# Reordering the last stage of a graph-attention layer with residual norm

## The chip, the cores and the metric

The kernel runs on one core of a Trainium2 chip. The core has TensorE (PE in the profile, with its weight loads as PEld), VectorE (DVE), ScalarE (ACT), GpSimd (POOL) and SyncE (SP), which here only issues transfers; 16 DMA engines move the data. The metric is the device time of one execution in microseconds. Before the change it is 236.07 us (median of 3 runs, 235.55 to 236.43).

## The reference

`x` is 4096 x 512, `adj` 4096 x 4096, both 32-bit floats. The layer is attention with four heads over the rows of `x`, with `adj` added to the scores, the mean over the heads, a residual and a norm over each row:

```python
ht = (h @ W).reshape(N, N_HEADS, N_HIDDEN).transpose(1, 0, 2)
...
e = jax.nn.leaky_relu(src[:, :, None] + dst[:, None, :], SLOPE) + adj_mat[None]
att = jax.nn.softmax(e, axis=-1)
h_prime = jnp.einsum('hij,hjd->hid', att, ht)
return h_prime.mean(axis=0)
...
x = _layernorm(x + _L0_gnn_ref(x, adj, L0_gnn_W, L0_gnn_a), axis=-1)
```

The entries of `adj` that are not zero go up to 1e9, so that in a row the largest entry decides the softmax by itself when it leads the second largest by more than the scores can differ. For such a row the result is `norm(x[i] + x[j] @ mean_h(W_h))`, where `j` is the column of the row's largest `adj`.

## The kernel before

The kernel computes that short form for all rows (`leading_rows`), bounds the scores from the norms of `x` and of the projected weights, counts the rows in which the lead is too small, and runs a full attention (`general`) only if there are any. With these inputs there are none, so the time is that of `leading_rows`.

The 4096 rows are 32 blocks of 128 rows, one row per partition. `NB` is 32, `KB` (parts of 128 of the 512 columns) is 4, `Q` is 4, `LATE` is 28 and `BEHIND` is 24. The schedule is written by hand: the order of the calls is the order on each engine's queue, and only semaphore waits are added to it.

A block passes these stages in the loop over `t`:

- `load_adj`: SP fetches the block's 2 MB of `adj`, five blocks ahead; the last block comes in four pieces. All loads and stores are on SP's queue, in the order of the calls, with at most eight under way.
- `segment_maxima`, `find_segment`: VectorE takes the maximum of each segment of 32 columns, then the largest segment maximum and its segment. GpSimd works out the segment's place (`row`, L174), gathers the segment from `adj` by an indirect transfer (`lead`, L176) and keeps the segment's first column (`start`, L181).
- `find_column`, two steps later: VectorE finds the column within the segment (L198), GpSimd adds the start (`col`, L200) and gathers the row of `x` for each partition (`y`, L186, in `gather_rows`). Block 31 doesn't go by its segment: `find_column_in_row` searches the whole row of 4096 (L206).
- `turn`, one step after that: TensorE transposes `y` in four parts (L213), ScalarE copies the result out of PSUM (`yt`, L215). `products` multiplies it by the mean of the heads' weights, four matmuls of 128x512 (L228), accumulating in PSUM.
- The residual. Up to block 23, `residual` (L221) adds `x` by a matmul with the identity, in the same PSUM tile. Blocks 24 to 27 are put by in SBUF (`put_by`, L241), and `add_x` (L244) adds their `x` later. Blocks 28 and 29 have a residual matmul at the start of step 31, and block 30 gets its `x` from VectorE (L511). Block 31 is kept as two half tiles, with `residual_in_halves` (L266) and `products_of_half` (L270).
- The norm. Either ScalarE makes the sums (`stats`, L250 and L252), GpSimd the inverse deviation (`rstd`, L255 to L257) and ScalarE the result (`finish`, L261), or, for the late blocks, VectorE makes `moments` (L281, L285), ScalarE a square root (L287), VectorE the inverse (`factor`, L290, L292) and the result (`normalise`, L297).

What is left after the loop is written out call by call (L463 to L525): the `x` norms of blocks 24 to 27 and ten stores of finished blocks, the search for blocks 30 and 31, then the products of blocks 28 to 31 between the norms of blocks 24 to 31 and the score bound (`bound(0)` to `bound(3)`, `test`, `count`, `report`), with the last six stores at the end. `store` is L313. A store of four blocks moves 8 KB per partition, one of two blocks 4 KB.

Of the kernel before, what the change touches and what calls it, by code (L numbers as in the profile page):

```python
# [10 lines left out]
U32 = mybir.dt.uint32  # L11
# [55 lines left out]
def leading_rows(ctx, tc, x, adj, W, a, out, ident, v, n_bad, any_bad):  # L67
# [100 lines left out]
    def find_segment(ib):  # L168
        seg = seg_of.pop(ib)
        nc.vector.max(out=top[:, ib, :], in_=seg)  # L170
        at = small.tile([P, 8], U32, name="at")
        nc.vector.max_index(at, top[:, ib, :], seg)  # L172
        row = small.tile([P, 1], U32, name="row")
        nc.gpsimd.tensor_tensor(row, at[:, 0:1], first[:, ib : ib + 1], op=OP.add)  # L174
        lead = lead_pool.tile([P, E], F32, name="lead")
        nc.gpsimd.indirect_dma_start(  # L176
            out=lead, out_offset=None, in_=adj_segs,
            in_offset=bass.IndirectOffsetOnAxis(ap=row[:, :1], axis=0),
        )
        start = at_of[ib] = small.tile([P, 1], U32, name="start")  # L180
        nc.gpsimd.tensor_tensor(start, at[:, 0:1], width, op=OP.mult)  # L181
        lead_of[ib] = lead

    def gather_rows(ib, col):
        y = y_t[ib] = y_pool.tile([P, D], F32, name="y")
# [8 lines left out]
    def find_column(ib):  # L194
        if ib < BEHIND:
            find_inner(ib)
        within = small.tile([P, 8], U32, name="within")
        nc.vector.max_index(within, top[:, ib, :], lead_of[ib])  # L198
        col = small.tile([P, 1], U32, name="col")
        nc.gpsimd.tensor_tensor(col, at_of.pop(ib), within[:, 0:1], op=OP.add)  # L200
        gather_rows(ib, col)
# [7 lines left out]
    def turn(ib):  # L209
        y = y_t.pop(ib)  # L210
        tp = psum.tile([P, KB, P], F32, name="tp", bufs=2)
        for kb in range(KB):
            nc.tensor.transpose(tp[:, kb, :], y[:, ts(kb, P)], ident)  # L213
        yt = yt_of[ib] = rows.tile([P, KB, P], F32, name="yt")
        nc.scalar.copy(yt, tp)  # L215

    def residual(ib):
        start = ib not in o_ps
        if start:
            o_ps[ib] = psum.tile([P, D], F32, name="o")  # L220
        nc.tensor.matmul(o_ps[ib], ident, hold[:, ib, :], start=start, stop=False)  # L221

    def products(ib, lo=0, hi=KB):
        start = ib not in o_ps
        if start:
            o_ps[ib] = psum.tile([P, D], F32, name="o")
        for kb in range(lo, hi):
            nc.tensor.matmul(  # L228
                o_ps[ib], yt_of[ib][:, kb, :], w_sum[:, kb, :],
                start=(start and kb == 0), stop=(kb == KB - 1),  # L230
            )
# [11 lines left out]
    def add_x(engine, ib):  # L243
        engine.tensor_add(hold[:, ib, :], hold[:, ib, :], o_ps["by"][:, ib - BEHIND, :])  # L244
        o_ps[ib] = hold[:, ib, :]

    def stats(ib):
        o, i = o_ps[ib], slice(ib, ib + 1)
        sq = rows.tile([P, D], F32, name="sq")
        nc.scalar.activation(sq, o, AF.Identity, scale=-1.0 / D, accum_out=nm[:, i])  # L250
        sq = rows.tile([P, D], F32, name="sq")
        nc.scalar.activation(sq, o, AF.Square, bias=nm[:, i], accum_out=sd[:, i])  # L252
# [6 lines left out]
    def finish(ib):  # L259
        i = slice(ib, ib + 1)  # L260
        nc.scalar.activation(hold[:, ib, :], o_ps.pop(ib), AF.Identity, bias=nm[:, i], scale=sd[:, i])  # L261

    def residual_in_halves(ib):
        o_ps[ib] = [psum.tile([P, D // 2], F32, name="o") for _ in range(2)]
        for k, o in enumerate(o_ps[ib]):
            nc.tensor.matmul(o, ident, hold[:, ib, ts(k, D // 2)], start=True, stop=False)  # L266
# [10 lines left out]
    def moments(ib):  # L277

        if ib < NB - 1:
            st = small.tile([P, nc.vector.BN_STATS_DIM], F32, name="st", bufs=2)  # L280
            nc.vector.bn_stats(st, o_ps[ib])  # L281
        else:
            st = halves_st
        mv = mean_var[ib] = small.tile([P, nc.vector.BN_AGGR_DIM], F32, name="mv", bufs=3)
        nc.vector.bn_aggr(mv, st)  # L285
        r = rt[ib] = sd[:, ib : ib + 1]
        nc.scalar.activation(r, mv[:, 1:2], AF.Sqrt, bias=eps)  # L287

    def factor(ib, shift=False):
        nc.vector.reciprocal(rt[ib], rt[ib])  # L290
        if shift:
            nc.vector.scalar_tensor_tensor(  # L292
                nm[:, ib : ib + 1], mean_var[ib][:, 0:1], -1.0, rt[ib], op0=OP.mult, op1=OP.mult
            )
# [17 lines left out]
    def store(queue, lo, n):  # L312
        queue.dma_start(out_rows[:, ds(lo, n), :], hold[:, ds(lo, n), :])  # L313
# [90 lines left out]
    vectors = [(kb, h) for kb in range(KB) for h in range(H)]  # L404
    vectors_at = {t: 2 if t < 3 else 1 for t in range(1, 15)}
    COLUMN, PROJECT, STATS, FINISH = 2, 3, 4, 6

    for t in range(NB):
        if t == NB // 2:
            tc.mark_branch_hint_location("general", engines=HINTED)  # L410
        if t in x_at:
            load_x(*x_at[t])
        if t + AHEAD == NB - 1:
            load_x(LATE, Q)
        load_adj(t + AHEAD)
        middle = 1 if t == NB - 1 else 2
        segment_maxima(t, 0, middle)
        if t >= COLUMN:
            find_column(t - COLUMN)
        segment_maxima(t, middle, PIECES)  # L420
        pair = FINISH <= t < BEHIND + FINISH and t % 2 == 0
        if pair:
            rstd(slice(t - FINISH, t - FINISH + 2))
        if t == NB - 1:
            for ib in (BEHIND, BEHIND + 2):
                load_x(ib, 2)
        find_segment(t)
        if t < 2:
            mean_of_heads(t)
        elif t == 2:  # L430
            mean_of_heads(2)
            mean_of_heads(3)
        if t == 0:
            turn_a()
        turned = [(*vectors[0], turn_w(*vectors.pop(0))) for _ in range(vectors_at.get(t, 0))]
        if t == 16:
            head_norms()
        ib = t - PROJECT
        if t == NB - 1:
            for late in range(LATE, NB):  # L440
                row_norm(late)
            residual(LATE)
            residual(LATE + 1)
        if ib >= 0:
            turn(ib)
            if ib > BEHIND:
                products(ib - 1, KB - 1, KB)
            if ib < BEHIND:
                residual(ib)
        for some in turned:  # L450
            head_vector(*some)
        if ib >= 0:
            products(ib, 0, KB if ib < BEHIND else KB - 1)
        if t >= BEHIND + STATS:
            put_by(t - STATS)
        elif t >= STATS:
            stats(t - STATS)
            row_norm(t - STATS)
        if pair:
            finish(t - FINISH)  # L460
            finish(t - FINISH + 1)

    for ib in range(BEHIND, LATE):  # L463
        row_norm(ib)
    for ib in range(0, 2 * Q, Q):
        store(nc.sync, ib, Q)
    for ib in range(2 * Q, BEHIND, 2):
        store(nc.sync, ib, 2)
    find_column(NB - 2)
    add_x(nc.gpsimd, BEHIND)  # L470
    add_x(nc.gpsimd, BEHIND + 1)
    find_column_in_row(NB - 1)
    add_x(nc.gpsimd, BEHIND + 2)
    products(LATE, KB - 1, KB)
    residual_in_halves(NB - 1)
    turn(NB - 3)
    products(NB - 3, 0, KB - 1)
    moments(LATE)
    for ib in range(BEHIND, NB):
        find_inner(ib)  # L480
    bound(0)
    products(NB - 3, KB - 1, KB)
    stats(BEHIND)
    factor(LATE)
    normalise(LATE, o_ps.pop(LATE))
    bound(1)
    turn(NB - 2)
    bound(2)
    add_x(nc.vector, LATE - 1)
    stats(BEHIND + 1)  # L490
    moments(LATE - 1)
    products(NB - 2, 0, 2)
    bound(3)
    test()
    pg = count()
    products(NB - 2, 2, KB - 1)
    stats(BEHIND + 2)
    rstd(slice(BEHIND, BEHIND + 2))
    rstd(slice(BEHIND + 2, BEHIND + 3))
    moments(NB - 3)  # L500
    report(pg)
    turn(NB - 1)
    factor(LATE - 1, shift=True)
    factor(NB - 3)
    normalise(NB - 3, o_ps.pop(NB - 3))
    finish(BEHIND)
    finish(BEHIND + 1)
    products(NB - 2, KB - 1, KB)
    products_of_half(NB - 1, 0)
    products_of_half(NB - 1, 1)  # L510
    nc.vector.tensor_add(hold[:, NB - 2, :], o_ps[NB - 2], hold[:, NB - 2, :])  # L511
    o_ps[NB - 2] = hold[:, NB - 2, :]
    moments(NB - 2)
    stats_of_half(NB - 1, 0)
    factor(NB - 2)
    normalise(NB - 2, o_ps.pop(NB - 2))
    finish(BEHIND + 2)
    finish(BEHIND + 3)
    stats_of_half(NB - 1, 1)
    moments(NB - 1)  # L520
    factor(NB - 1, shift=True)
    finish_in_halves(NB - 1)
    for ib, n in ((NB - 4, 1), (NB - 3, 1), (BEHIND, 2), (NB - 2, 1), (BEHIND + 2, 2)):
        store(nc.sync, ib, n)
    store(nc.sync, NB - 1, 1)  # L525

# [152 lines left out]
```

## Time and profile before

| | us |
|---|---|
| median of 3 runs | 236.07 |
| lowest, highest | 235.55, 236.43 |
| the profiled execution | 236.21 |
| its span, first to last instruction | 234.6 |
| PE busy (matmul) | 195.2 |
| DVE busy | 188.4 |
| ACT busy | 111.6 |
| POOL busy | 101.2 |

The span is the time between the first and the last instruction of the profiled execution; its own time has 1.6 us more, before and after it. Bytes moved: 97.21 MB, 414 GB/s over the span. The costliest groups of the page, with count, busy time and mean of one, then the idle time of the engine before them and who ended it:

```profile
L163 DVE TENSOR_REDUCE seg<-adj_t 128x64 f32<-128x2048 f32 (+1 forms) x68 | 146.0, 2149 | 32.7 <-DMA adj_t<-in_adj_dram 32.3
L228 PE MATMUL o<-w_sum,yt 128*128 128x512 f32 x248 | 115.1, 605 | 1.7 <-ACT yt L215 1.7
L176 POOL DMA_INDIRECT lead<-in_adj_dram,row x32 | 32.3, 1010 | 15.5 <-POOL row L174 15.0
L186 POOL DMA_INDIRECT y<-in_x_dram,col x32 | 30.9, 965 | 15.4 <-POOL col L200 15.2
```

A 128x512 matmul of 32-bit floats appears as two passes, so counts of L228 and its like are twice the calls. Matmuls overlap, so 605 ns is the length of one pass's record and not what one pass costs in a row of them.

### The profile page before, as it was taken

Reading aid. Unit: us, or ns where it says so; the run is one execution under the profiler, and the core shown is the slowest. Engines: PE = TensorE matmul, PEld = TensorE weight load, DVE = VectorE, ACT = ScalarE, POOL = GpSimd, SP = SyncE. Lnnn points to the kernel's source line nnn. Section 1 sums busy time; section 2 is a strip of 40 time slices with the busy share of each in tenths; the row PEclk is TensorE's granted clock in tenths of the full one; section 3 lists DMA queues with packets and bytes.
Section 4 is the critical chain, followed back from the end, with each engine's and each line's share of the span. In section 5 each row is a group of like instructions: output and inputs, shape, how many; then the busy total and the mean of one; then the engine's idle time right before and its main releaser. Section 6 shows DMA issues by size and latency. Waiting matters only on the chain.

```text
span 234.6 us, 2498 instructions
## 1 busy us (share of the span) xinstructions
PE 195.2 (83%) x683; PEld 101.4 (43%) x683; DVE 188.4 (80%) x302; ACT 111.6 (48%) x267; POOL 101.2 (43%) x215
## 2 busy tenths in 40 slices
PE   0188929999999999999979879797998968698990
PEld 0034514756565655555534333242443423244460
DVE  1736875589869995999589989998799999989672
ACT  2012011255474747474758354646464645166582
POOL 1012232414527462646353645464365464549130
PEclk9999977999999999999999999999799999999998
DMA  6999999999999999999999999999999999999985
GB/s 226 439 428 426 443 425 430 415 440 412 440 420 426 424 437 434 425 424 428 427 432 433 425 433 422 432 418 429 425 432 418 422 425 427 411 425 419 417 355 210
DMA packets 13697, 97.21 MB, mean 414 GB/s; under 512 B 2152, under 2 KB 2664, under 8 KB 7792
## 3 DMA queue, kind: packets, MB, share of 16 engines
q1 hardware_dynamic: 10080, 88.08, 88.9%
q0 software_dynamic: 3584, 8.92, 9.6%
q8 instruction: 6, 0.10, 0.2%
q14 instruction: 11, 0.09, 0.1%
q10 hardware_dynamic: 16, 0.02, 0.0%
HBM read 88.62 MB, written 8.39 MB: 414 GB/s over the span
## 4 chain that ended last, share of the span: by engine, by line
DMA 45%; POOL 17%; issue 15%; PE 10%; DVE 9%; ACT 1%; POOLq 0%; SPq 0%; DVEq 0%
DMA adj_t<-in_adj_dram 42%; DVE seg L163 8%; PE o L228 7%; POOL lead L176 6%; POOL y L186 5%; DMA y<-in_x_dram,col 3%; POOL sd L256 2%; PE o L270 2%; POOL start L181 1%; POOL row L174 1%; POOL col L200 1%; PE tp L213 1%; PE o L221 1%; ACT yt L215 1%; POOL sd L255 1%
## 5 line engine op out<-in xcount | busy, mean ns | idle before, releaser
L163 DVE TENSOR_REDUCE seg<-adj_t 128x64 f32<-128x2048 f32 (+1 forms) x68 | 146.0, 2149 | 32.7 <-DMA adj_t<-in_adj_dram 32.3
L228 PE MATMUL o<-w_sum,yt 128*128 128x512 f32 x248 | 115.1, 605 | 1.7 <-ACT yt L215 1.7
L228 PEld LDWEIGHTS o<-w_sum,yt 128*128 128x128 f32 x248 | 44.5, 191 | 54.8 <-issue 42.3
L215 ACT COPY yt<-tp 128x512 f32<-128x512 f32 x32 | 18.8, 588 | 44.3 <-PE tp L213 44.3
L176 POOL DMA_INDIRECT lead<-in_adj_dram,row x32 | 32.3, 1010 | 15.5 <-POOL row L174 15.0
L186 POOL DMA_INDIRECT y<-in_x_dram,col x32 | 30.9, 965 | 15.4 <-POOL col L200 15.2
L318 PE MATMUL o<-hold,ident 128*128 128x512 f32 x32 | 18.9, 745 | 17.5 <-DMA hold<-in_L_gnn_W_dram 17.5
L213 PE MATMUL tp<-ident,y 128*128 128x128 f32 x128 | 20.0, 280 | 12.6 <-DMA y<-in_x_dram,col 12.6
L221 PE MATMUL o<-hold,ident 128*128 128x512 f32 x52 | 27.3, 611 | 0.0
L213 PEld LDWEIGHTS tp<-ident,y 128*128 128x128 f32 x128 | 14.9, 143 | 25.4 <-issue 25.0
L174 POOL TENSOR_TENSOR row<-at,first 128x1 uint32<-128x1 uint32 x32 | 6.1, 190 | 42.0 <-DVE at L172 42.0
L336 ACT COPY wt<-tp 128x512 f32<-128x512 f32 x16 | 9.2, 587 | 31.4 <-PE tp L334 31.4
L200 POOL TENSOR_TENSOR col<-start,within 128x1 uint32<-128x1 uint32 x31 | 5.9, 190 | 40.1 <-DVE within L198 40.1
L235 ACT ACTIVATE sq<-hold 128x512 f32<-128x512 f32 x32 | 19.8, 619 | 0.0
L342 PEld LDWEIGHTS pv<-at_d,wt 128*128 128x128 f32 x128 | 16.3, 191 | 6.8 <-ACT wt L336 4.0
L318 PEld LDWEIGHTS o<-hold,ident 128*128 128x128 f32 x32 | 7.4, 243 | 26.7 <-POOL row L174 11.0
L319 ACT ACTIVATE w_sum<-o 128x512 f32<-128x512 f32 x4 | 2.4, 598 | 33.9 <-PE o L318 33.9
L261 ACT ACTIVATE hold<-o,nm,sd 128x512 f32<-128x512 f32 x24 | 17.2, 771 | 0.0
L252 ACT ACTIVATE sq<-o,nm 128x512 f32<-128x512 f32 x24 | 16.5, 688 | 0.8
L342 PE MATMUL pv<-at_d,wt 128*128 128x2 f32 x128 | 15.3, 244 | 0.6 <-ACT wt L336 0.6
L250 ACT ACTIVATE sq<-o 128x512 f32<-128x512 f32 x24 | 14.6, 609 | 0.0
L334 PEld LDWEIGHTS tp<-ident,hold 128*128 128x128 f32 x64 | 7.9, 142 | 6.9 <-issue 6.9
(85 smaller groups left out, 139.8 us busy)
## 6 DMA issues: line engine op xcount, KB each, us to landing
adj_t<-in_adj_dram SPq DMA_DIRECT2D x27, 2048.0 KB, 31.3
hold<-in_x_dram SPq DMA_DIRECT2D x7, 1024.0 KB, 33.2
adj_t<-in_adj_dram SPq DMA_DIRECT2D x6, 1024.0 KB, 25.7
out_dram<-hold SPq DMA_DIRECT2D x10, 512.0 KB, 15.2
adj_t<-in_adj_dram SPq DMA_DIRECT2D x8, 512.0 KB
hold<-in_L_gnn_W_dram SPq DMA_DIRECT2D x4, 1024.0 KB
out_dram<-hold SPq DMA_DIRECT2D x2, 1024.0 KB
hold<-in_x_dram SPq DMA_DIRECT2D x2, 512.0 KB, 14.1
```

What stands on the lines that cost most here:

```text
L163: nc.vector.tensor_reduce(seg_of[ib][:, ts(k, S // n)], adj_t[ib][:, ts(k, N // n)].rearrange("p (s e) -> p s e", e=E), axis=AX.X, op=OP.max,)
L176: nc.gpsimd.indirect_dma_start(out=lead, out_offset=None, in_=adj_segs, in_offset=bass.IndirectOffsetOnAxis(ap=row[:, :1], axis=0),)
L186: nc.gpsimd.indirect_dma_start(out=y, out_offset=None, in_=x, in_offset=bass.IndirectOffsetOnAxis(ap=col[:, :1], axis=0),)
L213: nc.tensor.transpose(tp[:, kb, :], y[:, ts(kb, P)], ident)
L215: nc.scalar.copy(yt, tp)
L221: nc.tensor.matmul(o_ps[ib], ident, hold[:, ib, :], start=start, stop=False)
L228: nc.tensor.matmul(o_ps[ib], yt_of[ib][:, kb, :], w_sum[:, kb, :], start=(start and kb == 0), stop=(kb == KB - 1),)
L235: nc.scalar.activation(sq, hold[:, ib, :], AF.Square, accum_out=xx[:, ib : ib + 1])
L252: nc.scalar.activation(sq, o, AF.Square, bias=nm[:, i], accum_out=sd[:, i])
L261: nc.scalar.activation(hold[:, ib, :], o_ps.pop(ib), AF.Identity, bias=nm[:, i], scale=sd[:, i])
L318: nc.tensor.matmul(o, ident, hold[:, w_at + kb * H + h, :], start=(h == 0), stop=(h == H - 1))
L342: nc.tensor.matmul(pv[:, kb, h : 2 * H : H], wt[:, k, :], at_d[:, k, h : 2 * H : H], start=(k == 0), stop=(k == KB - 1),)
```

## The change

All of it lies in the search for block 31 and in what follows the loop; the 31 steps before are as they were, instruction for instruction.

- `find_segment` is cut in two. The second half, `fetch_segment` (row, segment gather, start), is called at once for blocks 0 to 30. For block 31 it is called after block 30's column search, without the start, which nothing uses.
- Blocks 28 and 29 lose their residual matmuls. `add_residual` adds `x` on VectorE from PSUM into `hold`, as block 30 had it.
- The stores of blocks 0 to 3 and 4 to 7 no longer stand ahead of the two-block stores but among them (`HELD`).
- After block 31's search VectorE begins with the bound's maximum and block 28's addition and moments; the eight maxima of `find_inner` come after those. Block 28 is normalised by ScalarE (`finish`), and the moments of block 27 follow directly. Block 27's `x` is added by GpSimd, not by VectorE.
- On TensorE the transposes of blocks 29, 30 and 31 come earlier by one or two calls, and block 31's residual matmuls come behind block 29's transposes.
- Blocks 26 and 27 are finished by GpSimd (`finish_on_chip`), no longer by ScalarE.
- The last six stores change order: 28, 24-25, 26-27, 29, 30, 31. It was 28, 29, 24-25, 30, 26-27, 31.

```diff
     def find_segment(ib):
         seg = seg_of.pop(ib)
         nc.vector.max(out=top[:, ib, :], in_=seg)
-        at = small.tile([P, 8], U32, name="at")
+        at = at_of[ib] = small.tile([P, 8], U32, name="at")
         nc.vector.max_index(at, top[:, ib, :], seg)
+        if ib < NB - 1:
+            fetch_segment(ib)
+
+    def fetch_segment(ib):
+        at = at_of.pop(ib)
         row = small.tile([P, 1], U32, name="row")
         nc.gpsimd.tensor_tensor(row, at[:, 0:1], first[:, ib : ib + 1], op=OP.add)
...
-        start = at_of[ib] = small.tile([P, 1], U32, name="start")
-        nc.gpsimd.tensor_tensor(start, at[:, 0:1], width, op=OP.mult)
         lead_of[ib] = lead
+        if ib < NB - 1:
+            start = at_of[ib] = small.tile([P, 1], U32, name="start")
+            nc.gpsimd.tensor_tensor(start, at[:, 0:1], width, op=OP.mult)
...
+    def finish_on_chip(ib):
+        i, h = slice(ib, ib + 1), hold[:, ib, :]
+        o_ps.pop(ib)
+        nc.gpsimd.tensor_scalar(h, h, sd[:, i], nm[:, i], op0=OP.mult, op1=OP.add)
+
+    def add_residual(ib):
+        nc.vector.tensor_add(hold[:, ib, :], o_ps[ib], hold[:, ib, :])
+        o_ps[ib] = hold[:, ib, :]
...
+    HELD = ((8, 2), (10, 2), (12, 2), (0, Q), (14, 2), (16, 2), (Q, Q), (18, 2), (20, 2), (22, 2))
...
-            residual(LATE)
-            residual(LATE + 1)
...
-    for ib in range(0, 2 * Q, Q):
-        store(nc.sync, ib, Q)
-    for ib in range(2 * Q, BEHIND, 2):
-        store(nc.sync, ib, 2)
+    for ib, n in HELD:
+        store(nc.sync, ib, n)
     find_column(NB - 2)
+    fetch_segment(NB - 1)
     add_x(nc.gpsimd, BEHIND)
-    add_x(nc.gpsimd, BEHIND + 1)
     find_column_in_row(NB - 1)
-    add_x(nc.gpsimd, BEHIND + 2)
+    for ib in (LATE - 1, BEHIND + 1, BEHIND + 2):
+        add_x(nc.gpsimd, ib)
     products(LATE, KB - 1, KB)
+    turn(NB - 3)
     residual_in_halves(NB - 1)
-    turn(NB - 3)
     products(NB - 3, 0, KB - 1)
+    bound(0)
+    stats(BEHIND)
+    add_residual(LATE)
     moments(LATE)
+    bound(1)
+    factor(LATE, shift=True)
     for ib in range(BEHIND, NB):
         find_inner(ib)
-    bound(0)
+    turn(NB - 2)
     products(NB - 3, KB - 1, KB)
-    stats(BEHIND)
-    factor(LATE)
-    normalise(LATE, o_ps.pop(LATE))
-    bound(1)
-    turn(NB - 2)
+    finish(LATE)
+    moments(LATE - 1)
+    stats(BEHIND + 1)
     bound(2)
-    add_x(nc.vector, LATE - 1)
-    stats(BEHIND + 1)
-    moments(LATE - 1)
-    products(NB - 2, 0, 2)
     bound(3)
     test()
+    products(NB - 2, 0, 2)
     pg = count()
     products(NB - 2, 2, KB - 1)
     stats(BEHIND + 2)
     rstd(slice(BEHIND, BEHIND + 2))
     rstd(slice(BEHIND + 2, BEHIND + 3))
+    add_residual(NB - 3)
+    turn(NB - 1)
     moments(NB - 3)
     report(pg)
-    turn(NB - 1)
     factor(LATE - 1, shift=True)
     factor(NB - 3)
     normalise(NB - 3, o_ps.pop(NB - 3))
     finish(BEHIND)
     finish(BEHIND + 1)
+    finish_on_chip(BEHIND + 2)
+    finish_on_chip(BEHIND + 3)
...
-    nc.vector.tensor_add(hold[:, NB - 2, :], o_ps[NB - 2], hold[:, NB - 2, :])
-    o_ps[NB - 2] = hold[:, NB - 2, :]
+    add_residual(NB - 2)
...
-    finish(BEHIND + 2)
-    finish(BEHIND + 3)
...
-    for ib, n in ((NB - 4, 1), (NB - 3, 1), (BEHIND, 2), (NB - 2, 1), (BEHIND + 2, 2)):
+    for ib, n in ((LATE, 1), (BEHIND, 2), (BEHIND + 2, 2), (NB - 3, 1), (NB - 2, 1)):
         store(nc.sync, ib, n)
     store(nc.sync, NB - 1, 1)
```

## The prediction, made before the changed kernel ran

> **What bounds the kernel now.** I read the page's slices first, then the chain of waits over the last 31 us, then the busy times by stage, then the time lines of GpSimd and of the SP queue. The page's row of DMA slices settles the first 200 us:
>
> ```profile
> DMA  6999999999999999999999999999999999999985
> GB/s 226 439 428 426 443 425 430 415 440 412 440 420 426 424 437 434 425 424 428 427 432 433 425 433 422 432 418 429 425 432 418 422 425 427 411 425 419 417 355 210
> ```
>
> Every slice but the first and the last two is full, at about 425 GB/s. No byte is added or taken by the change, so only the end of the span can move. The chain of waits there:
>
> ```profile
> 203.58 0.63 PE tp L213 x4
> 204.21 3.57 PE o L228 x8
> 207.78 1.72 PE o L221 x4
> 209.49 0.44 PE tp L213 x4
> 209.93 4.38 PE o L228 x10
> 214.31 0.86 PE o L266 x4
> 215.17 0.45 PE tp L213 x4
> ...
> 216.28 2.84 PE o L228 x6
> ...
> 225.69 3.55 PE o L270 x16
> ...
> 230.69 0.56 ACT hold L310
> ```
>
> From 203.58 to 229.24 TensorE is the chain: residual matmuls (L221, L266), transposes (L213), products (L228, L270), broken only by two waits for ScalarE's copy of the turned rows. After the last product come 2.0 us of statistics and normalising, and at 231.29 the last store. The stages beside it (columns: stage; length; busy time of PE, PEld, DVE, ACT, POOL with counts; clock; DMA share; GB/s):
>
> ```profile
> 222.00:224.00 2.00, 2.00 (x7) 0.71 (x6) 1.60 (x9) 1.97 (x6) 1.11 (x3) 1.00 1.02 416
> 224.00:226.00 2.00, 2.00 (x9) 1.10 (x8) 1.34 (x4) 1.58 (x5) 0.93 (x3) 1.00 0.92 373
> 226.00:228.00 2.00, 2.00 (x11) 1.74 (x11) 1.76 (x5) 1.47 (x4) 0.00 (x0) 1.00 0.74 285
> 228.00:230.00 2.00, 1.23 (x6) 0.75 (x4) 1.22 (x4) 1.13 (x3) 0.00 (x0) 1.00 0.79 312
> 230.00:232.00 2.00, 0.00 (x0) 0.00 (x0) 0.78 (x3) 0.83 (x2) 0.00 (x0) 1.00 0.74 300
> 232.00:233.10 1.10, 0.00 (x0) 0.00 (x0) 0.00 (x0) 0.00 (x0) 0.00 (x0) 1.00 0.68 257
> ```
>
> The DMA engines are full until about 225 and then idle for 0.16 + 0.52 + 0.42 + 0.52 + 0.35 = 2.0 us in all. That sum is the second bound: however early TensorE ends, the transfers can't end more than 2.0 us sooner. GpSimd's time line shows the queue the change reorders:
>
> ```profile
> 210.41 0.97 POOL L176 DMA_INDIRECT lead<-in_adj_dram,row  x1 [0.51 <-PE tp L213]
> 212.00 0.97 POOL L186 DMA_INDIRECT y<-in_x_dram,col  x1 [0.27 <-POOL col L200]
> 212.99 2.50 POOL L244 TENSOR_TENSOR hold<-hold,adj_t 128x512 f32<-128x512 f32 x2
> 215.65 0.96 POOL L186 DMA_INDIRECT y<-in_x_dram,col  x1 [0.16 <-PE tp L213]
> ```
>
> Block 31's segment is fetched ahead of block 30's rows; block 31's rows wait for two adds. The trace's packet records give the landings (all 16 engines): rows of block 28 at 207.08, 29 at 212.61, 30 at 218.08, 31 at 222.25; a gather lands some 5.5 to 6.5 us after its issue begins, and TensorE takes it up 0.4 to 0.5 us later. In the same records the last backlogged store ends at 225.2 on the first DMA engine and only at about 227 on the last.
>
> [...]gather packets of 4 KB took 0.16 us, spaced out by store packets of 0.16 us (two-block stores) or 0.31 us (four-block stores), and the engines end up to 2 us apart. [...]The trace has the two-input form, 128x512 at 1.28 us[...]; the one-input form of that size it hasn't.[...] No row here shows a clash.
>
> **The change, part by part.**
>
> *Residuals of blocks 28, 29 by VectorE.* Two 128x512 matmuls (four passes) leave TensorE: −1.72 us on the chain at 207.78. Block 28's rows are there (207.08 + 0.45), so the transposes of 28 start at about 207.7 instead of 209.33 and their products end near 212.6 instead of 214.3. VectorE gains two additions of 0.69 us (L511's row); each then lets the normalising read SBUF, 0.55 instead of 0.81. VectorE was idle 1.81 us at 217.5 for the transposed bound, and 0.2 to 0.7 us four times later, which hides them. The block 28 normalising moves to ScalarE (0.80, a hold<-hold row of L261), in ScalarE's gap of 1.7 us before 219.58.
>
> *TensorE order.* The transposes of 29 now follow at once: 213.0, set by its rows (212.61 + 0.4), against 215.01. The two half residuals (0.86) go behind them, into the 0.65 us wait for the copy. Products of 29 then run 213.9 to 216.6 (2.7), and the bound's transpose follows. The transposes of 30 go ahead of the last product of 29, so that product (0.86) covers the next copy; but now TensorE stands waiting for block 30's rows.
>
> *GpSimd order.* Column and gather of 30 no longer stand behind row, segment gather and start of 31. Its column index is known at 210.35, so the issue starts at about 211.1 against 212.00: −0.9. With 5.5 to 6.5 us, landing is 217.2 ± 0.4, taken up at 217.7 ± 0.4. Four-block stores may lie beside this gather instead of block 29's: 4 packets per engine x 0.15 us = 0.6 at most, inside that spread. The segment of 31 is issued at about 212.8 and lands near 217.6 (4.8 us, as now); it is wanted only for the eight maxima, which I place at 217.4 to 218.5. One add (1.28) stands ahead of block 31's gather instead of two, and it fits before the index arrives (214.88): issue at 215.3 against 215.65, landing 221.8.
>
> *TensorE from there.* Transposes of 30 at 217.8; + 0.45 + 0.86 (last product of 29) + 0.2 (bound) + 2.0 (two products of 30, with fill) + 0.15 (count) + 0.9 (third product) = 222.3, where 31's rows are ready (221.8 + 0.45). Transposes 0.45 and the last product of 30 0.86 give 223.6. ScalarE must have copied 31's rows: it passes the moments of 24, 25 and 26 (1.56 each), the last two from 219.9 to 223.0, and the copy ends at 223.6, level. Half products 3.55: end 227.2 against 229.24, **−2.0 us**. VectorE, adding and measuring block 30 from 224.65 on, reaches the first half's statistics at 226.3 and the second's at 227.4: 0.15 late. The last store is issued at about 229.4 instead of 231.29.
>
> *GpSimd finishes blocks 26, 27.* No row shows a one-input 128x512.[...] by the two-input row 1.3 at most.[...] ScalarE's last moment pass ends at 223.0, the three small steps take 1.1 as now, so both are done by 225.8 (226.8 at 1.3).[...] ScalarE is freed of 1.5 us there.
>
> *Stores.* The sixteen stores are the same bytes; the first ten only change order among themselves. At the end the order becomes 28, 24-25, 26-27, 29, 30, 31, issued by my times at (backlogged), 225.5, 225.9, 226.2, 227.5, 229.4. A store's first packet comes 0.83 us after issue; eight packets per engine take 1.27 (two blocks) or 0.65 to 0.8 (one). An early DMA engine is then free at 230.3 and takes the last store at 230.25: 230.9. A late one ends 28 at 227.0: + 1.27 + 1.27 + 3 x 0.65 = 231.5. And one late engine also fetches 16 KB of instructions, 1.01 us at 227.71 in the trace; in it the end was 233.01 with no idle time behind that fetch. If it keeps that load, it ends at about 232.5.
>
> **Sum.** Chain −2.0, of which the transfers can follow by 0.5 (loaded engine) to 1.5 (the others): −1.0 taken. The profiled execution took 236.21, 1.6 around its span of 234.6, and lies 0.14 above the median of 236.07; 236.21 − 1.0 = **235.2**.
>
> **Rivals.** *A, full gain:* the fetch hits an early engine or an idle moment, and the end follows to 1.5 us: 234.6. For it: most engines idle 2.0 us now. Against: the last landing is that of the slowest of 16. *B, nothing:* the loaded engine has the same bytes and no idle time now, or block 30's gather lands 1.5 us late and TensorE, which now blocks on it before the last product of 29, gives the gain back: 236.0. For it: the 1.01 us packet sits on the path to 233.01. *C, slower:* the store of 26-27 stands ahead of 29, 30 and 31 on SP's queue and waits for GpSimd. If a one-input 128x512 takes c, that store is issued at 224.2 + 2c, and the end is 0.83 + 1.27 + 3 x 0.65 = 4.05 later. At c = 2.4 this reaches 233.0, no gain; from c = 3.0 it is slower by over 1.2; at c = 3.3 the end is 234.8, 1.8 later: 238.0. Against it: 1.28 for the dearer two-input form. *D, the order doesn't do what it says:* two-block stores first merely swap which gather meets the four-block packets; worth under 0.6 us either way, in the range.
>
> **Chances.** Forecast 0.46, A 0.22, B 0.17, C 0.15. This kernel's runs tell 0.5% (1.2 us) from no change, so "faster" means under 234.9: nearly all of A and a fifth of the forecast, 0.30. "Slower" is over 237.25: C and a little of B's tail, 0.17. Same: 0.53. Range: A less 0.3 below, 234.3; above, B with 0.7 for a gather or lock clash, 236.7; C lies outside.
>
> **What would show it.** Right: transposes of block 28 at 207.7 and 29 at 213; the last half product ending near 227; the last store issued by 229.6; DMA share over 0.9 from 226 to 230. Wrong in the chain: TensorE waiting over 2 us for block 30's rows, or the statistics of the first half starting after 227. Wrong in GpSimd: L272 over 1.3 us. Wrong in the transfers: last landing still at 233 with the last store issued before 230.

## The result, and the profile after

The changed kernel takes 237.33 us (median of 12 runs, 236.63 to 239.08) against 235.69 (12 runs, 235.53 to 236.43): a ratio of 1.0066, 95% interval 1.0047 to 1.0085. It is 1.6 us slower, where 0.9 us faster was forecast, and the median lies above the range of 234.3 to 236.7. The profiled execution took 236.93, its span is 235.4. Calls and names are the same, but lines have moved: transposes are L219, products L234, half products L285, GpSimd's additions L250, the shift `nm` of `factor` L307.

The page's DMA slices after, to be held against the row of before that the prediction shows:

```profile
DMA  6999999999999999999999999999999999999956
GB/s 241 436 432 415 443 420 432 423 432 418 435 432 416 425 442 424 425 425 427 441 426 429 429 432 420 433 412 437 426 434 412 426 425 420 418 419 419 419 233 266
```

The body is as it was; the slice before the last has fallen to 233 GB/s. The chain of waits of the changed kernel over its last 30 us (start, length, what):

```profile
211.01 7.65 DMA y<-in_x_dram,col
218.66 0.14 issue
218.80 0.84 PE tp L219 x4
219.64 1.71 PE o L234 x2
221.35 0.51 PE px L390 x2
221.86 2.24 PE o L234 x4
...
225.30 0.44 PE tp L219 x4
225.74 0.86 PE o L234 x2
226.60 3.55 PE o L285 x16
```

TensorE is no longer the chain throughout. It waits for the gather of block 30's rows, which takes 7.65 us from issue to the transposes, and then one product (two passes) takes 1.71 us where the same product took 0.86 before. The stages say why (stage; length; busy times of PE, PEld, DVE, ACT, POOL; clock; DMA share; GB/s):

```profile
218.00:220.00 2.00, 1.20 (x5) 1.01 (x6) 2.00 (x1) 0.32 (x1) 2.00 (x2) 0.77 1.04 433
220.00:222.00 2.00, 2.00 (x5) 0.71 (x4) 1.74 (x12) 1.26 (x4) 0.08 (x1) 0.50 1.01 418
222.00:224.00 2.00, 2.00 (x4) 0.68 (x4) 1.86 (x10) 1.97 (x7) 0.36 (x2) 0.88 1.01 410
...
226.00:228.00 2.00, 2.00 (x9) 1.43 (x8) 1.34 (x4) 1.96 (x4) 1.86 (x3) 1.00 0.23 90
228.00:230.00 2.00, 2.00 (x10) 1.53 (x9) 1.87 (x5) 0.29 (x1) 0.00 (x0) 1.00 0.64 252
```

Three things stand out. The granted clock is down to half for 3.41 us from 219.07 on. The DMA engines, at 0.74 in stage 226 to 228 before, are at 0.23: the next store in SP's order, that of blocks 24 and 25, went out only at 227.99. And in stage 218 to 220 VectorE is busy for 2.00 us with a single instruction. VectorE's time line has it:

```profile
217.06 0.14 DVE L305 RECIPROCAL sd<-sd 128x1 f32<-128x1 f32 x1
217.24 2.87 DVE L307 SCALAR_TENSOR_TENSOR nm<-mv,sd 128x1 f32<-128x1 f32 x1
220.03 0.83 DVE L198 MAX8 inner<-lead 128x8 f32<-128x32 f32 x8
...
225.19 0.16 DVE L307 SCALAR_TENSOR_TENSOR nm<-mv,sd 128x1 f32<-128x1 f32 x1
```

The shift of block 28, one element per partition, takes 2.87 us; the same instruction for block 27 takes 0.16. GpSimd's time line over the same stretch:

```profile
213.45 1.28 POOL L250 TENSOR_TENSOR hold<-hold,adj_t 128x512 f32<-128x512 f32 x1
215.40 0.96 POOL L192 DMA_INDIRECT y<-in_x_dram,col  x1 [0.67 <-issue]
216.38 3.70 POOL L250 TENSOR_TENSOR hold<-hold,adj_t 128x512 f32<-128x512 f32 x3
...
226.21 1.77 POOL L272 TENSOR_SCALAR hold<-hold,sd,nm 128x512 f32<-128x512 f32 x2
```

The three additions run back to back from 216.38 to 220.08, and the shift ends at 220.11; such additions without a gap are called a train below. The shift, with two inputs in SBUF, stops (2.87 us), while the one-input reciprocal, 0.18 us earlier and also beside an addition, doesn't (0.14). Begun during the first addition, the shift got in after the third, not after the first. That it waited for GpSimd's additions, called the lock below, is at this point the author's reading of two time lines; the experiments test it.

So there were three suspects: the lock, the late rows of block 30, the halved clock.

### The profile page after: what moved, and what is told of

The parts are those of the page before. It is cut to its first block, busy times and chain, and to the rows that moved or that the text cites. A ratio compares the mean times of both kernels' runs of the same rounds, so it can differ in the third digit from the quotient of the medians.

```text
span 235.4 us, 2490 instructions
## 1 busy us (share of the span) xinstructions
PE 193.8 (82%) x679; PEld 100.0 (42%) x679; DVE 190.6 (81%) x303; ACT 111.1 (47%) x266; POOL 103.7 (44%) x217
## 4 chain that ended last, share of the span: by engine, by line
DMA 34%; issue 22%; POOL 22%; PE 14%; DVE 4%; ACT 2%; POOLq 0%; SPq 0%; DVEq 0%
DMA adj_t<-in_adj_dram 16%; DMA hold<-in_L_gnn_W_dram 11%; POOL lead L181 7%; POOL y L192 7%; PE o L234 5%; DMA y<-in_x_dram,col 3%; DMA lead<-in_adj_dram,row 3%; DVE seg L163 3%; PE o L333 3%; POOL sd L262 2%; PE o L285 2%; PE pv L357 1%; POOL row L179 1%; POOL start L188 1%; POOL col L206 1%
## 5 line engine op out<-in xcount | busy, mean ns | idle before, releaser
L234 PE MATMUL o<-w_sum,yt 128*128 128x512 f32 x248 | 115.9, 609 | 0.7 <-ACT yt L221 0.7
L234 PEld LDWEIGHTS o<-w_sum,yt 128*128 128x128 f32 x248 | 44.6, 192 | 52.7 <-issue 41.2
L219 PE MATMUL tp<-ident,y 128*128 128x128 f32 x128 | 19.9, 279 | 16.2 <-DMA y<-in_x_dram,col 16.2
L333 PE MATMUL o<-hold,ident 128*128 128x512 f32 x32 | 18.7, 738 | 17.4 <-DMA hold<-in_L_gnn_W_dram 17.4
L219 PEld LDWEIGHTS tp<-ident,y 128*128 128x128 f32 x128 | 14.4, 142 | 30.2 <-issue 30.1
L227 PE MATMUL o<-hold,ident 128*128 128x512 f32 x48 | 24.6, 594 | 0.0
```

The source lines that it names most:

```text
L234: nc.tensor.matmul(o_ps[ib], yt_of[ib][:, kb, :], w_sum[:, kb, :], start=(start and kb == 0), stop=(kb == KB - 1),)
L333: nc.tensor.matmul(o, ident, hold[:, w_at + kb * H + h, :], start=(h == 0), stop=(h == H - 1))
```

## Experiments

Each ratio is to the kernel before on the same chip, with its 95% interval; the medians of before were 236.13, 235.99, 236.34 and 236.09 on the four chips used.

**e1: the changed kernel with block 28's shift made by ScalarE.** Two ScalarE instructions take the place of the one on VectorE; nothing else changes.

```diff
+    def shift_on_scalar(ib):
+        nc.vector.reciprocal(rt[ib], rt[ib])
+        minus = small.tile([P, 1], F32, name="minus", bufs=1)
+        nc.scalar.activation(minus, mean_var[ib][:, 0:1], AF.Identity, scale=-1.0)
+        nc.scalar.activation(nm[:, ib : ib + 1], minus, AF.Identity, scale=rt[ib])
...
-    factor(LATE, shift=True)
+    shift_on_scalar(LATE)
```

> The changed kernel, but block 28's shift (minus mean times inverse deviation) made by two ScalarE instructions instead of VectorE's one with two SBUF inputs. Lock theory (VectorE's 2.87 us instruction at 217.24 waited for GpSimd's three adds[...]): no VectorE instruction over 1 us after 215 except the row search; the eight maxima start by 217.8 instead of 220.03; ScalarE's moments of block 25 start near 219 to 220 instead of 221.91; the copy of block 31's rows no longer waits for ScalarE. Time: 0.3 to 1.0 us less where the clock stays full, little where TensorE's clock halves. Clock theory: no change, 237.3. Rival (VectorE waited for a semaphore[...]): the stall stays in another instruction.

236.30 us, ratio 1.000 (0.9979 to 1.0021). All that the change lost is back, by one 128x1 instruction put elsewhere. No instruction of VectorE stalls; its maxima began at 219.04 and not by 217.8, since the transposed bound that stands ahead of them came late from TensorE. Its VectorE time line beside the train of additions, which here runs from 216.88 to 220.59 (L317 is the reciprocal in the new function):

```profile
218.97 0.14 DVE L317 RECIPROCAL sd<-sd 128x1 f32<-128x1 f32 x1
219.04 0.81 DVE L198 MAX8 inner<-lead 128x8 f32<-128x32 f32 x8
219.78 0.66 DVE L296 BATCH_NORM_STATS2 st<-hold 128x6 f32<-128x512 f32 x1
```

The maxima and the statistics, of one SBUF input each, run at their usual length beside the additions: 0.81 us for the eight maxima and 0.66 for the statistics, against 0.83 and 0.67 in the profile after, where they come behind the train.

**a1: the changed kernel again, and e8: the train one addition shorter.** In e8 VectorE adds block 27's `x`, as before the change.

```diff
-    for ib in (LATE - 1, BEHIND + 1, BEHIND + 2):
+    for ib in (BEHIND + 1, BEHIND + 2):
...
+    add_x(nc.vector, LATE - 1)
     moments(LATE - 1)
```

> The changed kernel once more, beside the next three. Theory (the lock costs about 1.5 us and stands in nearly every execution): 1.006 times before, and a division of about 2.5 to 3 us in the profile, ending with the third addition. Rival (the first profile's clash was a chance of that execution): the division takes 0.2 us here.

> The changed kernel with block 27's addition given back to VectorE, where it was before, so that GpSimd's train behind block 31's gather has two additions of 1.28 us and not three; VectorE works 0.7 us more before block 27's moments. Theory (the shift waits until the train's end): the train ends 1.25 us earlier, the stalled shift ends near 218.8 in place of 220.1, and the time falls to about 1.003 times before (236.6), between the changed kernel and e1. Rival (only the last of the additions matters, or the lock is not the cause): no change against the changed kernel.

a1: 237.56 us, ratio 1.0041 (1.0021 to 1.0062). e8: 236.91, ratio 1.0026 (0.9998 to 1.0055), as its theory had it, though the interval reaches 1 and the two times aren't told apart; what tells them apart is when the shift ends. The instruction that the expectation of a1 calls a division is the shift; it took 1.40 us, not 2.5 to 3, because it came later, and it ended with the third addition. The shift of e8 ended at 219.62, in a profile in which block 29's gather was issued 0.79 us later than in after. The chain of waits of a1 is the clearest view of the lock's price:

```profile
218.46 0.28 DVE xg L386
218.74 0.08 DVE sd L305
218.82 0.02 issue
218.85 0.05 DVE nm L307
218.90 1.27 issue
220.17 0.84 DVE inner L198 x8
...
222.83 0.19 DVE gap L405
223.02 0.04 issue
223.06 0.22 PE px L409 x2
```

Here VectorE is the chain: 1.27 us in which it waits for nothing that the profile names, then the maxima, the moments of block 27 and the bound, and TensorE stands 1.12 us at the count (L409) for them. In the same stages of a1 the granted clock is 1.00 from 216 to 232, and the execution took 236.97, as long as the first one with the halved clock (236.93).

**e5: one addition more,** into a tile that nothing reads.

```diff
         add_x(nc.gpsimd, ib)
+    spare = rows.tile([P, D], F32, name="spare", bufs=1)
+    nc.gpsimd.tensor_add(spare, hold[:, 0, :], hold[:, 1, :])
```

> The changed kernel with a fourth addition of 128x512 on GpSimd right behind its three, into a tile that nothing reads. Lock theory[...]: VectorE's stalled instruction ends with the fourth add, 1.27 us later than in the changed kernel, the moments of blocks 25 and 26 move as much, and the time rises by 0.8 to 1.3 us, to 238.1 to 238.6. Rivals (clock, gather, order of the last stores): GpSimd is idle there for 3.5 us, so the fourth add costs nothing and the time stays at 237.3.

239.13 us (6 runs), ratio 1.0118 (1.0078 to 1.0157): by the ratios 1.2 us over the changed kernel in its first runs and 1.8 over a1, more than the lock theory's 0.8 to 1.3. Its VectorE time line and, below, GpSimd's:

```profile
218.86 3.54 DVE L307 SCALAR_TENSOR_TENSOR nm<-mv,sd 128x1 f32<-128x1 f32 x1
```

```profile
217.46 3.71 POOL L250 TENSOR_TENSOR hold<-hold,adj_t 128x512 f32<-128x512 f32 x3
221.13 1.25 POOL L488 TENSOR_TENSOR spare<-hold 128x512 f32<-128x512 f32 x1
```

The shift now ends with the fourth addition. That addition shares no tile with the shift, so a wait for data isn't the reason. (This execution took 242.15 us, 3.0 over that kernel's median, so only these lines are read from it.) In all six profiles in which it meets the train:

| | shift starts | takes | ends | last addition ends |
|---|---|---|---|---|
| e8 (two additions) | 218.10 | 1.52 | 219.62 | 219.59 |
| after (three) | 217.24 | 2.87 | 220.11 | 220.08 |
| a1 (three) | 218.85 | 1.40 | 220.25 | 220.22 |
| e2 (three) | 219.49 | 1.43 | 220.92 | 220.88 |
| e3 (three) | 220.14 | 1.13 | 221.27 | 221.24 |
| e5 (four) | 218.86 | 3.54 | 222.40 | 222.38 |

How long it stands depends on when it comes; when it ends is fixed by the train. With none, two, three and four additions in its way the ratios are 1.000, 1.003, 1.004 to 1.007, 1.012.

**e2 and e6: the order of the stores.** e2 is the changed kernel with both four-block stores behind the two-block ones; e6 is e1 with block 29's store ahead of the pairs.

```diff
-    HELD = ((8, 2), (10, 2), (12, 2), (0, Q), (14, 2), (16, 2), (Q, Q), (18, 2), (20, 2), (22, 2))
+    HELD = ((8, 2), (10, 2), (12, 2), (14, 2), (16, 2), (18, 2), (20, 2), (22, 2), (0, Q), (Q, Q))
```

```diff
-    for ib, n in ((LATE, 1), (BEHIND, 2), (BEHIND + 2, 2), (NB - 3, 1), (NB - 2, 1)):
+    for ib, n in ((LATE, 1), (NB - 3, 1), (BEHIND, 2), (BEHIND + 2, 2), (NB - 2, 1)):
```

> The changed kernel with both four-block stores behind all two-block stores. Gather theory (4 KB packets of block 30's rows wait behind 8 KB store packets): the rows of block 30 need 1.4 to 1.7 us from first to last packet instead of 2.74 and land by 217.4 instead of 218.37; TensorE takes them up at 217.8 instead of 218.80; its idle wait is 1.0 us instead of 2.0, the half clock becomes rarer; time 0.5 to 1.5 us less. Lock theory alone: TensorE starts earlier but the copy of 31's rows still waits for ScalarE until about 225, so at most 1.0 less. If store sizes do not matter: landing and time as in the changed kernel.

> Block 28's shift on ScalarE, as in e1_nolock, and the store of block 29 ahead of those of 24-25 and 26-27. Theory of the pile at the end: block 29 is ready 0.6 us before blocks 24-25 and waits for them on SP's queue; now the DMA engines start on it at once, the last landing comes 0.3 to 0.6 us sooner than in e1_nolock, time 0.2% under it and under the kernel before. Rival (the last landing is set by TensorE's end and one late DMA engine): equal to e1_nolock, ratio 1.000.

e2: 237.56, ratio 1.0058 (1.0041 to 1.0074), like the changed kernel: the gather theory's gain didn't come. e6: 236.05, ratio 0.9997 (0.9977 to 1.0018), like e1. Neither order makes a difference that can be measured.

**e3, e4, e10: idle transposes ahead of block 30's,** so that TensorE doesn't stand still: 16 in the changed kernel (e3), 16 with e1's and e2's edits (e4), 6 with e1's edit (e10).

```diff
+        for k in range(fill):
+            nc.tensor.transpose(tp[:, k % KB, :], hold[:, 0, ts(k % KB, P)], ident)
...
-    turn(NB - 2)
+    turn(NB - 2, fill=16)
```

> The changed kernel with 16 idle transposes (results overwritten) on TensorE ahead of block 30's transposes, where it waits 2.0 us for the rows. Clock theory (the wait lets the granted clock fall to 0.5 for 3.4 us): the clock is 1.0 from 216 to 230 in the profile, the last product of 29 takes 0.86 instead of 1.71, half products end 1.0 to 1.4 us earlier, and the run-to-run spread shrinks to under 1 us; median 236.0 to 236.6. Lock theory: ScalarE's copy of 31's rows still waits for the moments until about 225, so no more than 1.0 us is gained. If the clock is not the cause: no gain, or 0.1 to 0.2 more.

> All three edits together. [...]TensorE's half products end near 227.5 as predicted for the change, the last store is issued at 229.5 to 230, and the time is 234.6 to 235.4, below the kernel before. If a fourth cause holds (last stores queued behind the store of blocks 24 and 25), half products end early but the last landing stays at 233 or later: 235.7 to 236.5.

> e1 with six idle transposes (about 0.7 us) ahead of block 30's, to keep TensorE from standing still for 2 us. Theory (the halved clock after the wait costs up to 1.4 us in some executions of e1): no stretch of clock 0.5 between 218 and 226, and the time 0.3 to 0.8 us under e1, ratio 0.997 to 0.999. Rival (the clock doesn't drop in most executions of e1, or its loss is hidden behind the last transfers): within 0.2 us of e1, or slower by the filler's own length.

e3: 237.28, ratio 1.0052 (1.0032 to 1.0072); none of its products was slowed (the two passes at 221.74 took 1.02 us, as in e1, where the profile after has 1.91) and the time didn't fall. e4: 236.95, ratio 1.0027 (1.0002 to 1.0051), above e1 and above both of its forecasts. In e3's profile the fillers took 1.9 us and stood in the way, because block 29 was late. In e4's own profile they didn't: they were done at 219.63, and the transposes behind them waited 0.48 us more for the rows. Why e4 is above e1 stays open. e10: 236.13, ratio 0.9994 (0.997 to 1.0017), level with e1. Since e3's fillers may cost what they gain, the better evidence against the clock is a1, whose profiled execution was as slow at a clock of 1.00 from 216 to 232, and e1, level with before: the halved clock is not why the median rose. That it costs something where it comes is seen in single executions: 0.85 us on one product in the profile after.

**e7 and b0: before, with the residuals of blocks 28 and 29 on VectorE as the only edit (e7), and before unchanged (b0).**

```diff
-            residual(LATE)
-            residual(LATE + 1)
...
+    add_residual(LATE)
     moments(LATE)
...
+    add_residual(NB - 3)
     moments(NB - 3)
```

> The kernel before with one part of the change: the residuals of blocks 28 and 29 added by VectorE and not by TensorE. Theory that the matmuls taken from the chain are the real gain and the gathers of 29 to 31 have 1.9 to 2.4 us of slack there: half products end 1.3 to 1.7 us earlier than in the kernel before, last landing 0.5 to 1.0 earlier, ratio 0.996 to 0.998. Rival (the transfers set the end, or the gathers take the slack): ratio 1.000. If VectorE's 1.4 us more delay its later work: half products early but the last store not, ratio 1.000 to 1.003.

> The kernel before, unchanged, beside the others on this chip. Every theory: ratio 1.00 within 0.3%. Its profile gives, on the same chip, where block 29's gather starts and how late the gathers of 29 to 31 land, against which the tails of the others are read.

e7: 236.03, ratio 1.0005 (0.9985 to 1.0026). b0: 235.89, ratio 0.9997 (0.9972 to 1.0022). In both profiles block 28's rows landed at about 208.1 to 208.3, not 207.1, and its transposes began at 208.78 (e7) and 209.01 (b0). There the two residual matmuls had been done in a wait: taking them away takes nothing off the chain.

**e9, e11, e12, and a2: what is left of the change.** a2 is e1 again. e9 is e1 with the old order of the last two fetches. e11 is e1 with blocks 26 and 27 finished by ScalarE and the last stores as before; e12 is e11 with the old order of the fetches.

```diff
-        if ib < NB - 1:
-            fetch_segment(ib)
+        fetch_segment(ib)
...
-    fetch_segment(NB - 1)
```

```diff
-    finish_on_chip(BEHIND + 2)
-    finish_on_chip(BEHIND + 3)
...
     normalise(NB - 2, o_ps.pop(NB - 2))
+    finish(BEHIND + 2)
+    finish(BEHIND + 3)
...
-    for ib, n in ((LATE, 1), (BEHIND, 2), (BEHIND + 2, 2), (NB - 3, 1), (NB - 2, 1)):
+    for ib, n in ((LATE, 1), (NB - 3, 1), (BEHIND, 2), (NB - 2, 1), (BEHIND + 2, 2)):
```

> e1 (no lock) with the old order of the two last fetches on GpSimd: block 31's segment ahead of block 30's rows. The gather of 30 is issued about 1.0 us later (212.0 to 212.5). Theory (TensorE, now without slack, waits on block 30's rows, and the end follows TensorE in part): 0.3 to 0.9 us slower than e1, ratio 1.002 to 1.004. Rival (the last transfers hold the end, and TensorE's end has slack before them): within 0.2 us of e1, ratio 0.999 to 1.001, with TensorE's end later by about 0.5 to 1.0.

> e1 once more (block 28's shift by ScalarE), beside the next two. Both theories: 0.998 to 1.002 times before. In the profile, if GpSimd's finishing of blocks 26 and 27 overlaps VectorE's normalising of block 29, that one takes 1.0 us in place of 0.55.

> e1 with blocks 26 and 27 finished by ScalarE behind block 30's square root, as before the change, and the last stores in the old order. GpSimd then has nothing beside VectorE's normalising of blocks 29 and 30. Theory (the second clash stood on the path): normalising of 29 takes 0.55, the last statistics follow TensorE's last matmul by 0.05 or less, 0.3 to 0.5 us under e1, ratio 0.997 to 0.999. Rival 1 (the last transfers hold the end): TensorE and the last store earlier, the time within 0.2 us of e1. Rival 2 (ScalarE's 1.5 us of finishing stands in the way of block 31's square root): slower than e1 by 0.2 to 0.5.

> e11 with the old order of the fetches (block 31's segment ahead of block 30's rows). What remains of the change is TensorE's order, the residuals of 28 and 29 on VectorE, the train of three additions and the stores held between. Theory: block 30's rows are taken up 0.3 to 0.7 us later than in e11, and the end 0.2 to 0.5 later. Rival (block 30's rows aren't what TensorE's end waits for, since the late landings decide): within 0.2 us of e11.

e9: 236.27, ratio 1.0013 (0.9988 to 1.0039). a2: 235.99, ratio 0.9994 (0.9979 to 1.001). e11: 236.04, ratio 0.9994 (0.9981 to 1.0006). e12: 236.43, ratio 1.0015 (0.9998 to 1.0032). The profiles of e3, e4, e6, e9 and e10 show a second, short clash: block 29's normalising beside GpSimd's finishing takes 1.00 us and not 0.55. In those of after, a1, e1 and a2 it takes 0.55 to 0.56. Taking the finishing away from GpSimd (e11) gains nothing that can be measured. The order of the fetches may be worth 0.2% (e9 and e12 both above their partners), inside the intervals. None of these beats the kernel before.

## Why the prediction was wrong

Times of profiles are best laid over each other at the issue of block 29's gather (206.05 in before, 206.06 in after), since what comes ahead of it shifts by over 1 us from one profile to the next (205.85 in e7, 207.29 in e3). From there on, with the prediction's own times less 206.05:

| us | transposes 28 | 29 | 30 | 31 | last half product ends | last store issued |
|---|---|---|---|---|---|---|
| before | 3.28 | 8.96 | 13.88 | 18.18 | 23.18 | 25.24 |
| b0 (before again) | 2.89 | 8.60 | 13.52 | 17.82 | 22.82 | 24.88 |
| predicted | 1.65 | 6.95 | 11.75 | 16.25 | 21.15 | 23.35 |
| after | 1.50 | 6.50 | 12.73 | 19.08 | 24.07 | 26.13 |
| a1 (after again) | 1.46 | 7.91 | 12.00 | 17.91 | 23.04 | 25.09 |
| e1 | 1.58 | 7.84 | 11.94 | 16.66 | 21.65 | 23.71 |
| a2 (e1 again) | 1.55 | 7.90 | 12.00 | 16.72 | 21.72 | 23.77 |

1. **The step that failed: the lock, put at nothing for the shift.** Block 28's move to ScalarE needs a shift from VectorE, which before was made for blocks 27 and 31 only. The prediction has no term for it; it put VectorE's added work into idle time ("which hides them") without asking what GpSimd did then. Its range had 0.7 for "a gather or lock clash" in all, the author's estimate, with no row of before behind it for the lock. The shift took 2.87 and 1.40 us where an undisturbed one takes 0.16, and with it gone from VectorE the ratio falls from 1.0066 and 1.0041 to 1.000 and 0.9994. That before shows no clash of the two engines says little. These are lines of before, GpSimd's and then VectorE's:

```profile
216.63 1.29 POOL L244 TENSOR_TENSOR hold<-hold,adj_t 128x512 f32<-128x512 f32 x1
```

```profile
219.48 0.67 DVE L244 TENSOR_TENSOR hold<-hold,adj_t 128x512 f32<-128x512 f32 x1
...
223.93 0.16 DVE L292 SCALAR_TENSOR_TENSOR nm<-mv,sd 128x1 f32<-128x1 f32 x1
```

None of its VectorE additions and shifts with two tensors in SBUF fell beside GpSimd's additions (212.99 to 215.49, 216.63 to 217.92). GpSimd's finishing beside VectorE's normalising of block 29 cost less: in the profile after, the normalising took its 0.55 and GpSimd's second finishing 1.01 instead of 0.77; in those of e3, e4, e6, e9 and e10 the normalising took about 0.46 more.
2. **What the stall delayed.** The moments of blocks 25 and 26 on ScalarE, forecast for 219.9 to 223.0, ran from 221.91 to 224.93, because ScalarE's queue has block 27's square root ahead of them. Behind them in the queue stand the copy of block 31's rows and then the finishing of blocks 24 and 25. In a1 the copy follows the moments directly: the store of 24 and 25 went out at 227.16, and the DMA share from 226 to 228 was 0.32, against 226.13 and 0.77 in e1. The bound's count was late in a1 as well: from block 30's transposes to block 31's it takes 5.91 us there and 4.72 in e1, and TensorE ends 1.4 us later (23.04 against 21.65). In the profile after, TensorE came later still, held by block 30's rows and the halved clock, so that there the wait that ended last was this one and not the stall:

```profile
225.78 0.58 ACT L221 COPY yt<-tp 128x512 f32<-128x512 f32 x1 [0.85 <-PE tp L219]
```

3. **TensorE's chain without the lock: right.** e1 and a2 lie within 0.6 us of the predicted row in every column but block 29's transposes (0.9 late; the last packets of its rows came at 213.24 in a2, 213.69 in e1).
4. **Block 30's gather: forecast to land at 217.2 ± 0.4.** The forecast counts to the signal behind the last packet, which came 0.16 us after it in before and 0.39 in after. In a1 and a2 the last packets came at 217.20 and 217.27, in e1 at 217.76, where all of it is 0.57 later (206.63 for 206.06). In after they came at 217.98: by the packet records 60 of its 64 packets were there at 216.87, and a 16 KB packet of the instruction queue took 0.92 us from 216.10 on. The records don't name the engine; that this packet held one of the 16, whose share is four packets, is inferred. That fetch falls within one of the last five gathers in every profile (at 211.19 in a1, 211.81 in e1, 206.21 in b0, 201.21 in before), and makes that one about 1 us late. The prediction counted only another such fetch, at the end of the transfers, which came as well (228.19), and none here, where the change had taken away some 2 us of slack between landing and use. A late gather of block 30 is also one half of rival B; it came in this profile and not in a1.
5. **GpSimd's finishing: 0.77 and 1.01 us against 0.8.** The 0.8, which is what the forecast's 225.8 for the end of both comes to by its own 224.2 + 2c, was the author's estimate; no row of before shows it. The size was right for the undisturbed one. Rival C was wrong: its point, 3.0, was not come near.
6. **How much the end follows TensorE: overrated.** This is the second step that failed: the sum took 1.0 us from the end, and without the lock nothing measurable is left of it. With the lock gone TensorE ends 1.1 to 1.5 us earlier than in before and b0, and the last store goes out as much earlier, but it lands 2.5 us after its issue in e1 and a2, against 1.7 in before and b0. The profiled e1 took 235.98 and a2 235.52, before 236.21 and b0 235.80; the medians are level. This is the outcome of rival B; its reason, "the loaded engine has the same bytes", fits but wasn't tested. That the late landings and the transfers' end share the rest of the gain is argued from these profiles; how much each takes was not separated.

So the change has two halves: a shorter TensorE chain that is worth nothing measurable at the end, and a lock that costs 0.4 to 0.7%. The chance of 0.17 for slower had been given to another mechanism.

## What to carry to other kernels

Where an edit moves work to GpSimd, or moves GpSimd's work in time, list every VectorE instruction with two SBUF inputs that can start beside it, however small: here the price of the shift was not its own 0.16 us but what was left of GpSimd's train of additions (1.13 to 3.54 us in all), and all of VectorE's queue stood behind it. The runs show this for the 128x1 shift alone; that the two inputs are what matters was not shown by itself. Time gained on one engine needs a second look at the transfers on both of its sides: the gathers that it now waits for, and the stores that must follow. A chain of waits from one execution can name a real but occasional loss (here the halved clock) and leave out the steady one; a second profile of the same kernel and an edit that removes one suspect are cheap.

## What the runs showed of the hardware

- A 128x1 VectorE instruction with two SBUF inputs, 0.16 us undisturbed, waited until a back-to-back train of two, three or four 128x512 additions on GpSimd was over (1.13 to 3.54 us in six profiles), and ended 0.02 to 0.04 us after it; by the records, which are rough for GpSimd, the next addition begins 0.04 to 0.05 us before the last one ends.
- A VectorE normalising of 128x512 from SBUF (one tensor, two values per partition) that began 0.04 us after the first of two finishings on GpSimd took 1.00 us against 0.55 alone. It did not wait for the end of both: in e6 it ended at 227.27, the second finishing at 227.90. Where it began ahead of them (a1, e1, a2) it took 0.55 to 0.56 and the first finishing 0.81 to 0.85 instead of 0.76; where it began 0.58 us into the first one (after), it took 0.55 and the second finishing 1.01. With its tensor in PSUM it took 0.81 beside an addition (before, at 216.66), as it did at 224.68, with no addition beside it.
- After TensorE had waited 1.98 us for block 30's rows, the clock was halved for 3.41 us, from 219.07 to 222.48. In before it was halved for 3.41 us from 164.84 on, after a wait of 2.16. The length of the wait doesn't settle it: in the first of these executions the clock stayed at 1.00 through a wait of 2.20 us that ended at 176.63. In e11 TensorE waited 2.47 us for block 28's rows, and the ten product passes behind them took 5.79 us, against 4.38 in b0 (mean granted clock of the executions 0.960 and 0.993). In a2, where block 30's transposes follow the products of 29 without a wait, the product behind them took 0.86 us, as in before at a clock of 1.00.
- A 16 KB packet of the instruction queue took 0.92 to 0.97 us beside one of the last five gathers, and the last packet of the gather that it met came 0.9 us (e10) to 1.5 us (e3) behind the 60th of its 64 (1.1 in before and after).
